# Correlation copies on two engines, a top-k choice in two pieces, and the next queries' turn behind the outputs

## The chip, the cores and the metric

The kernel runs on one core of a Trainium2 chip. The core has five engines that take their instructions in order and wait for each other through semaphores: TensorE (PE in the profile, with its weight loads shown apart as PEld), VectorE (DVE), ScalarE (ACT), GpSimd (POOL) and SyncE (SP), which here only issues DMAs. The metric is the device time of one execution in microseconds (us).

## The reference

The input x is 8 batches of 128 tokens with 512 features, and there is a context of the same shape. Two decoder layers run, each of three sublayers; after every one the input is added and layer-normalised:

```python
x = _layernorm(x + _L0_attn_ref(x, ...))       # 32 heads of 16, causal, with biases
x = _layernorm(x + _L0_xattn_ref(x, ctx, ctx)) # autocorrelation, 8 heads of 64
x = _layernorm(x + _L0_ffn_ref(x, ...))        # 28 experts of rank 8, the best 2
x = _layernorm(x + _L1_attn_ref(x, ...))       # 32 heads, q and k layer-normalised, ALiBi
x = _layernorm(x + _L1_xattn_ref(x, ctx, ...)) # 16 query heads on 4 key heads of 96
x = _layernorm(x + _L1_ffn_ref(x, ...))        # routed low-rank sum
```

The second of these is the one that the first two parts of the change touch. For every feature it takes the circular correlation of queries and keys over the 128 tokens, picks the 9 largest values of the 128, and adds the values shifted by the places found, weighted by a softmax:

```python
corr = jnp.fft.ifft(qf * jnp.conj(kf), axis=2).real
w, idx = jax.lax.top_k(corr.transpose(0, 1, 3, 2), topk)
w = jax.nn.softmax(w, axis=-1)
for i in range(topk):
    g = jnp.minimum(idx[:, :, None, :, i] + pos, L - 1)
    out = out + w[:, :, None, :, i] * jnp.take_along_axis(v, g, axis=2)
```

The fourth (second attention, `_L1_attn_ref`) is the one that the third part touches.

## The kernel before

Everything is in fp32. One batch is one tile: 128 tokens on the partitions and 512 features along them. The Tile framework's list scheduler takes the program in its order of issue and sets the order of the instructions on each engine by their dependencies, priorities and costs; on the chip each engine then works through its own list in order. What stands in which order in the source therefore shifts several lists at once.

**First attention, 0 to 225 us.** Batches go in pairs, four pairs of four groups of eight heads: sixteen steps (p, f), n = 0 to 15 (L515). A step computes scores (s_a L165), adds the causal mask (e_a L370, two instructions, one for each half of the rows), takes maxima (m_a L182) and exponentials (`exps`, L194) in two halves. Then the step before the previous one gives its outputs (`turned.out()`, o_a L244 and L250, into oT L258), the queries and keys of the next step are projected, the previous step's exponentials are transposed (`prev.turn()`, pt_a L225, copied as pT_a L226), and a piece of the correlation is done (`auto`, L505). Output projections (po, L86) and the layer norms stand in between.

**The correlation.** Class `Correlated` handles a pair of batches. `spectra` makes the products of the spectra, `correlate` transforms them back (pc L418, on a pair of PSUM banks) and copies them (co L423); `chosen(h)` finds for batch h of the pair the nine largest of 128 in each of four rows with MAX8 and MATCH_REPLACE8 (top, wk, nxt, L434 to L440) and makes the softmax weights (ex, su, rcw, L441 to L449); `shifted(h)` transposes the weights (wT, through pt_wT L129) and multiplies spectra (pvf L459, pw L463, wf L468, vw L471 and L473); `done(h)` transforms back (poc) and adds and normalises (x_c). The pieces of the pairs 0 and 1 are spread over places (n, 0) and (n, 1) of the attention's steps, two places a step, pair p from step 7 + 4p on (L500 to L503). Those of the pairs 2 and 3 (`third`, `fourth`) stand in a hand-written list among the experts (L716 to L761, 225 to 345 us).

**Second attention, 345 to 500 us.** A loop over the batches b (L832), each in two halves f = 0 and f = 2. A half computes scores, adds the ALiBi bias (e_a L703), takes maxima and exponentials (`exps(0)`, `exps(1)`), lets the previous half give its outputs (`turned.out()`), makes the next batch's raw queries (q L648), values or keys, transposes the previous half's exponentials, and divides (`divide`, rc_a L205 on VectorE, e_a L208 on GpSimd). For f = 2 `turned_queries(b + 1)` turns the next batch's normalised queries (q L652): four transposes into one PSUM bank (pTq L676) and four ScalarE activations that scale and shift (qT L678). `turned_tokens` makes the transposed tokens xTa (L139). The projection of the previous batch ends in x_a (L103), its layer norm comes later (`late`, L107).

Cross-attention and the last sublayer follow from 500 us on; the change does not touch their source.

Of the kernel before, what the change touches and what calls it, by code (L numbers as in the profile page):

```python
# [11 lines left out]
F32 = mybir.dt.float32  # L12
# [5 lines left out]
P = 128  # L18
B, S, D = 8, 128, 512
NC = D // P  # L20
# [8 lines left out]
BIG = -1e30  # L29
# [9 lines left out]
def bc(ap, shape):  # L39
    return ap.to_broadcast(shape)  # L40
# [3 lines left out]
def decoder(ctx: ExitStack, tc: tile.TileContext, a: dict, out: bass.AP):  # L44
    nc = tc.nc
# [4 lines left out]
    sm = ctx.enter_context(tc.tile_pool(name="sm", bufs=4))  # L50
# [3 lines left out]
    def stage(name, bufs, side=None):  # L54
        return tc.tile_pool(name=name, bufs=bufs, side=side, reuse_waits="tile")

    def bank(name):
        return ps1.tile([P, 512], F32, tag="ps1", name=name)

    def banks(name):  # L60
        return ps2.tile([P, 2, 512], F32, tag="ps2", name=name)
# [55 lines left out]
    def catch_up(behind=None):  # L117

        with tc.issue_after(behind.ins) if behind and late else nullcontext():
            while late:  # L120
                late.pop(0)()
# [161 lines left out]
    cp = autos.enter_context(stage("c0", 1, side="right"))  # L283
# [59 lines left out]
    def values(p, j):  # L343
        v, vd = vs[p, j] = v_bufs[(2 * p + j) % 4]
        pv = bank(f"pv0_{p}_{j}")
        mm_acc(pv, [(xts[p][:, c, j * P : (j + 1) * P], wv[:, c, :]) for c in range(NC)])
        by_head = lambda t: t.rearrange("p (a x d) -> p a x d", x=2, d=HD)
        nc.vector.tensor_tensor(padded(v), by_head(pv), by_head(bqkv[:, 0, :]), ALU.add)
        first_keys(vd, v)
# [33 lines left out]
    class Correlated:  # L383
# [27 lines left out]
        def correlate(self):  # L411
            pc = banks(f"pc_{self.p}")
            for i in range(NC):
                cols = slice(i * P, (i + 1) * P)
                for n in range(2):
                    for h in range(2):
                        rows = slice(64 * h, 64 * h + 64)
                        nc.tensor.matmul(  # L418
                            pc[:, h, cols], lhsT=self.pr[n][rows, 0, cols],
                            rhs=dft[rows, T_I + n * P : T_I + (n + 1) * P], start=(n == 0), stop=(n == 1),  # L420
                        )
            self.co = cp.tile([P, 2, NC, P], F32, tag="co", name=f"co_{self.p}")
            nc.scalar.copy(self.co.rearrange("p h c t -> p h (c t)"), pc)  # L423

        def chosen(self, h):

            b, co = self.bs[h], self.co[:, h]

            top = sm.tile([P, NC, 8], F32, tag="top", name=f"top_{b}")
            nxt = sm.tile([P, NC, 8], F32, tag="nxt", name=f"nxt_{b}")  # L430
            wk1 = cp.tile([P, NC, P], F32, tag="wk1", name=f"wk1_{b}")
            wk2 = cp.tile([P, NC, P], F32, tag="wk2", name=f"wk2_{b}")
            for i in range(NC):
                nc.vector.max(top[:, i, :], co[:, i, :])  # L434
                nc.vector.match_replace(wk1[:, i, :], top[:, i, :], co[:, i, :], BIG)
                nc.vector.max(nxt[:, i, :], wk1[:, i, :])

            nc.vector.memset(nxt[:, :, TOPK - 8 :], BIG)
            for i in range(NC):
                nc.vector.match_replace(wk2[:, i, :], nxt[:, i, :], wk1[:, i, :], BIG)  # L440
            ex = cp.tile([P, NC, P], F32, tag="ex", name=f"ex_{b}", bufs=2)  # L441
            nc.gpsimd.tensor_tensor(ex, co, bc(top[:, :, 0:1], [P, NC, P]), ALU.subtract)
            nc.scalar.activation(ex, ex, AF.Exp)
            nc.vector.scalar_tensor_tensor(ex, wk2, BIG, ex, ALU.is_equal, ALU.mult)
            su = sm.tile([P, NC], F32, tag="su", name=f"su_{b}")
            nc.vector.tensor_reduce(su, ex, AX.X, ALU.add)
            rc = sm.tile([P, NC], F32, tag="rcw", name=f"rcw_{b}")
            nc.vector.reciprocal(rc, su)
            nc.gpsimd.tensor_tensor(ex, ex, bc(rc.unsqueeze(2), [P, NC, P]), ALU.mult)  # L449
            self.ex[h] = ex  # L450
# [32 lines left out]
        def pieces(self):  # L483

            return [
                [self.spectra], [],
                [self.correlate], [lambda: self.chosen(0)],
                [lambda: self.shifted(0)], [lambda: self.chosen(1)],
                [lambda: self.done(0), lambda: self.shifted(1)], [],
                [lambda: self.done(1)],  # L490
            ]


# [21 lines left out]
    for n, (p, f) in enumerate(steps):  # L515
        if f == 0:
            oTs.append(ap.tile([P, 2, NC, P], F32, tag="oT", name=f"oT0_{p}"))
        qT, kbd = qk
# [117 lines left out]
    def turned_tokens(b):  # L636
        xT = qp.tile([P, NC, P], F32, tag="xT", name=f"xTa1_{b}")
        transposed(xs[b], NC, P, xT, f"xTa1_{b}", "a")
        return xT

    def normed(i, b, xT, later=None):


        n, w = (("q", w1q), ("k", w1k))[i]
        pq = bank(f"p{n}1_{b}")
        mm_acc(pq, [(xT[:, c, :], w[:, c, :]) for c in range(NC)])
        q = qp.tile([P, D], F32, tag=n, name=f"{n}1_{b}")
        nc.vector.tensor_scalar(q, pq, 8.0, -8.0, ALU.min, ALU.max)  # L648
        mean, rs = moments(q, f"{n}1_{b}")

        def normalized():
            done = nc.vector.tensor_scalar(q, q, mean, rs, ALU.subtract, ALU.mult)  # L652
            if i:
                nc.gpsimd.tensor_tensor(q, q, lnv[:, 0, :], ALU.mult)
                nc.gpsimd.tensor_tensor(q, q, lnv[:, 1, :], ALU.add)
            return done

        if later is None:
            normalized()
        else:  # L660
            later.append(normalized)
        return q
# [9 lines left out]
    def turned_queries(b, q):  # L672
        qT = ap.tile([P, NC, P], F32, tag="qT", name=f"qT1_{b}")
        pt = bank(f"pTq1_{b}")
        for c in range(NC):
            nc.tensor.transpose(pt[:, c * P : (c + 1) * P], q[:, c * P : (c + 1) * P], ident)  # L676
        for c in range(NC):
            nc.scalar.activation(  # L678
                qT[:, c, :], pt[:, c * P : (c + 1) * P], AF.Identity, scale=lnq[:, 0, c : c + 1], bias=lnq[:, 1, c : c + 1]
            )  # L680
        return qT
# [19 lines left out]
    def alibi_bias(f):  # L701
        def bias(e, s, r0):
            return nc.vector.tensor_tensor(e, s, alibi[:, f // 2, r0], ALU.add)  # L703

        return bias
# [43 lines left out]
    raw = [normed(i, 0, xT) for i in range(2)]  # L749
# [82 lines left out]
    for b in range(B):  # L832
        qT, kbd = qk
        v_now = v
        oT = ap.tile([P, NC, P], F32, tag="oT", name=f"oT1_{b}")
        for f in (0, 2):
            units = []
            for i in (f, f + 1):
                feats = slice(i * P, (i + 1) * P)
                units.append((qT[:, i, :], kbd[:, :, feats], v_now[0][:, i * 192 : (i + 1) * 192], v_now[1][:, i * 128 : (i + 1) * 128]))  # L840
            now = Heads16(ap, units, alibi_bias(f), oT[:, f : f + 2, :], f"a1_{b}_{f}", keys_late)
            if f == 2 and b + 1 < B:

                qT = turned_queries(b + 1, raw[0])
            now.exps(0)
            catch_up(now.scored)

            if turned:
                turned.out()
            if b + 1 < B:  # L850
                if f == 0:
                    raw = [normed(0, b + 1, xT)]
                else:
                    v = values(b + 1, xT)
                    if b + 2 < B:
                        xT = turned_tokens(b + 2)
            if b == 0:
                E(7) if f == 0 else None
            if b == B - 1:
                front.go(1)  # L860
            if prev:
                prev.turn()
            now.divide(0)
            now.exps(1)
            half = projection(b - 1, oT_before) if f == 2 and b else iter((0, 0))
            next(half)
            if b + 1 < B:
                if f == 0:
                    raw.append(normed(1, b + 1, xT, keys_late))
                else:  # L870
                    qk = qT, turned_keys(b + 1, raw[1])
            now.divide(1, turned_keys.done if f == 2 and b + 1 < B else None)
            if b == B - 1:
                front.go(1)
            next(half)
            turned, prev = prev, now
        oT_before = oT
# [12 lines left out]
    with stage("x1b", 2, side="right") as ap, stage("f1", 2, side="right") as fp:  # L890
# [164 lines left out]
        nxt, upcoming = Front(1), None  # L1055
# [41 lines left out]
        for b in range(B):  # L1097
            pr, j = divmod(b, 2)
            if j == 0 and b:
                front, nxt = nxt, upcoming  # L1100
# [222 lines left out]
```

## Time and profile before

| | us |
|---|---|
| median of 3 runs | 887.82 (887.67 to 888.66) |
| the profiled execution | 888.51 |
| its span, first to last instruction | 886.7 |
| TensorE busy in the span | 852.5 |
| VectorE busy | 562.8 |
| ScalarE busy | 370.2 |
| GpSimd busy | 189.0 |

The profile is that of one execution. Its span leaves out 1.8 us that lie around the first and the last instruction. The list of waits puts each wait of an engine down to the instruction that ended it. The chain of waits goes back from the last instruction of a stretch, at each step to what released it or to the instruction before it on its engine. In the timeline a row is one or several instructions of the same kind, with start, length, engine and line, what it writes and reads, and in brackets the idle time of the engine before it with what ended it. The granted clock (PEclk) is 1.00 at full speed; the mean over the span is 0.995.

### The profile page before, as it was taken

To read this page: it belongs to the slowest core of one execution; us is meant where nothing else is said; L and a number is where in the kernel's file an instruction comes from. 1 tells how busy PE (TensorE), PEld (TensorE's weight loads), DVE (VectorE), ACT (ScalarE), POOL (GpSimd) and SP (SyncE) were. 2 spreads that over 40 slices of the span, in tenths; PEclk is the share of its full clock that TensorE was granted. 3 is DMA by queue.
4 is the path that set the end of the run, shared out by engine and by line. 5 is a ranking of instruction groups with operands and counts; after the bars stand their busy time and mean duration, and the time that the engine had idled before them with its cause. 6 is when DMAs were issued, how large, how long until landed. Compare 5 with 4: busy or idle time off the path is not lost.

```text
span 886.7 us, 16971 instructions
## 1 busy us (share of the span) xinstructions
PE 852.5 (96%) x6454; PEld 524.6 (59%) x6454; DVE 562.8 (63%) x1329; ACT 370.2 (42%) x1534; POOL 189.0 (21%) x267
## 2 busy tenths in 40 slices
PE   9999999999899999999999999999999999999996
PEld 5766655754445454555555688758475846576442
DVE  3756797776968658788888621735363545467654
ACT  3787474564222116766666603213122322224310
POOL 2400233132243224555555300000000000000000
PEclk9999999999999999999999999999999999999998
DMA  9800000130300002000004020332113211313340
GB/s 331 322 2 25 2 13 13 49 108 1 131 0 25 1 0 96 2 1 2 2 1 143 27 72 1 70 89 45 41 36 92 45 47 36 82 42 78 83 94 35
DMA packets 30067, 50.68 MB, mean 57 GB/s; under 512 B 5537, under 2 KB 22049, under 8 KB 28193
## 3 DMA queue, kind: packets, MB, share of 16 engines
q1 hardware_dynamic: 27424, 47.49, 18.0%
q10 hardware_dynamic: 2560, 2.10, 1.1%
q8 instruction: 51, 0.84, 0.4%
q14 instruction: 32, 0.25, 0.1%
HBM read 30.69 MB, written 2.10 MB: 37 GB/s over the span
## 4 chain that ended last, share of the span: by engine, by line
PE 63%; DVE 20%; ACT 11%; POOL 2%; issue 1%; DMA 1%; SPq 0%; ACTq 0%; POOLq 0%; DVEq 0%
PE pqx L86 9%; PE pox L974 8%; ACT e_a L194 7%; PE pkx L86 4%; PE pvx L86 4%; PE s_x L912 4%; PE pof L86 4%; PE o_x L957 4%; PE pq L86 3%; PE pk L86 3%; DVE e_a L703 3%; PE pv L86 3%; DVE m_a L182 3%; PE pt_a L225 2%; PE pw L463 1%
## 5 line engine op out<-in xcount | busy, mean ns | idle before, releaser
L194 ACT ACTIVATE e_a<-e_a,m_a 128x128 f32<-128x128 f32 (+1 forms) x512 | 184.7, 364 | 93.6 <-DVE m_a L182 93.6
L933 ACT ACTIVATE e_x<-s_x,m_x 128x256 f32<-128x256 f32 x128 | 58.7, 484 | 140.2 <-DVE m_x L923 122.8
L194 ACT ACTIVATION_READ_ACCUMULATOR e_a<-e_a,m_a 128x1 f32 x512 | 96.8, 189 | 0.0
L974 PE MATMUL pox<-w_X_o,oTx 128*128 128x512 f32 x192 | 84.9, 596 | 1.0 <-DVE oTx L963 1.0
L86 PE MATMUL pqx<-xTx,w_X_q 128*128 128x256 f32 x384 | 84.9, 380 | 0.0
L86 PEld LDWEIGHTS pqx<-xTx,w_X_q 128*128 128x128 f32 x384 | 72.6, 190 | 11.4 <-issue 1.8
L922 DVE TENSOR_REDUCE m_x<-s_x 128x4 f32<-128x1024 f32 x32 | 37.6, 1217 | 41.2 <-PE s_x L912 41.2
L974 PEld LDWEIGHTS pox<-w_X_o,oTx 128*128 128x128 f32 x192 | 35.7, 190 | 46.4 <-issue 44.3
L182 DVE TENSOR_REDUCE m_a<-e_a 128x4 f32<-128x512 f32 (+1 forms) x128 | 62.6, 541 | 0.0
L97 POOL TENSOR_TENSOR rs_x<-ve_x,neghalf 128x1 f32<-128x1 f32 x7 | 3.8, 549 | 269.4 <-DVE ve_x L95 250.4
L208 POOL TENSOR_TENSOR e_a<-e_a,rc_a 128x512 f32<-128x512 f32 x64 | 51.8, 827 | 44.0 <-DVE rc_a L205 19.9
L225 PE MATMUL pt_a<-ident,e_a 128*128 128x128 f32 x384 | 48.7, 274 | 4.9 <-DVE e_a L370 3.9
L225 PEld LDWEIGHTS pt_a<-ident,e_a 128*128 128x128 f32 x384 | 43.4, 140 | 12.9 <-DVE e_a L370 4.9
L912 PE MATMUL s_x<-kTx,qTx 32*128 32x256 f32 x768 | 50.0, 385 | 1.0 <-ACT e_x L933 1.0
L912 PEld LDWEIGHTS s_x<-kTx,qTx 32*128 32x128 f32 x768 | 39.0, 184 | 17.1 <-issue 11.7
L957 PE MATMUL o_x<-pT_x,vx 128*32 128x512 f32 x384 | 43.7, 595 | 1.8 <-issue 0.6
L941 DVE STREAM_TRANSPOSE e_x<-e_x 128x1024 f32<-128x1024 f32 x32 | 39.7, 1241 | 0.8
L940 DVE TENSOR_SCALAR e_x<-e_x,rc_x 128x256 f32<-128x256 f32 x128 | 36.3, 347 | 4.2 <-DVE rc_x L937 2.5
L103 DVE TENSOR_TENSOR x_x<-pox,x_a 128x512 f32<-128x512 f32 x7 | 4.8, 686 | 52.5 <-PE pox L974 52.5
L823 ACT COPY qTx<-pqx 128x512 f32<-128x512 f32 x24 | 14.1, 595 | 55.5 <-PE pqx L86 55.5
L165 PEld LDWEIGHTS s_a<-kbd,qT 32*64 32x64 f32 x1024 | 20.7, 131 | 27.7 <-issue 12.7
L165 PE MATMUL s_a<-kbd,qT 32*64 32x256 f32 (+1 forms) x1024 | 33.2, 335 | 2.1 <-DVE pT_a L226 1.1
(223 smaller groups left out, 1611.8 us busy)
## 6 DMA issues: line engine op xcount, KB each, us to landing
pT_x<-e_x SPq DMA_DIRECT2D x224, 64.0 KB, 2.0
w_X_q<-in_X_q SPq DMA_DIRECT2D x3, 1024.0 KB, 4.8
w_X_o<-in_X_o SPq DMA_DIRECT2D x3, 1024.0 KB, 4.7
w_L_Wv<-in_L_Wv SPq DMA_DIRECT2D x2, 1024.0 KB, 6.3
w_L_Wo<-in_L_Wo SPq DMA_DIRECT2D x2, 1024.0 KB, 7.5
x_in<-in_x SPq DMA_DIRECT2D x8, 256.0 KB, 8.2
ct<-in_ctx SPq DMA_DIRECT2D x8, 256.0 KB, 4.4
cT<-in_ctxT SPq DMA_DIRECT2D x4, 512.0 KB, 4.0
```

The costliest lines, as they stand in the source:

```text
L86: nc.tensor.matmul(ps, lhsT=l, rhs=r, start=(i == 0), stop=(i == n - 1))
L165: nc.tensor.matmul(s[r // 2][64 * u : 64 * u + 64, r % 2, cols], lhsT=qT[rows, 64 - 64 * part : P - 64 * part], rhs=kbd[rows, :, :keys], s ...
L182: self.scored = nc.vector.tensor_reduce(self.m[:, part, rs, :], self.by_heads(part)[:, rs], AX.X, ALU.max, negate=True)
L194: nc.scalar.activation(e[:, r, x, :], e[:, r, x, :], AF.Exp, bias=self.m[:, part, r, x : x + 1], accum_out=self.su[:, part, r, x : x + 1],)
L208: nc.gpsimd.tensor_tensor(e, e, bc(self.rc[:, part, rs, :].unsqueeze(3), list(e.shape)), ALU.mult)
L225: nc.tensor.transpose(pt[:, r, cols], self.e[:, 2 * i + r, cols], ident)
L912: nc.tensor.matmul(sc[g // 2][:, g % 2, u * 256 : (u + 1) * 256], lhsT=qT[rows, (h0 + u) * NS + n, :], rhs=kT[rows, n], start=(n == 0), st ...
L922: nc.vector.tensor_reduce(m, self.s[i], AX.X, ALU.max, negate=True)
L933: nc.scalar.activation(self.e[:, :, j, :], self.s[half][:, i, :].rearrange("p (a k) -> p a k", k=32), AF.Exp, bias=self.m[:, j : j + 1], s ...
L941: nc.vector.transpose(self.e[:, :, js, :], self.e[:, :, js, :])
L957: nc.tensor.matmul(po[32 * g : 32 * g + 32, :], lhsT=v[:, s, g * XD + 32 * n : g * XD + 32 * n + 32], rhs=pT[:, s].rearrange("p i h x -> p ...
L974: nc.tensor.matmul(po, lhsT=oT[:, n, h * P : (h + 1) * P], rhs=w, start=(i == 0), stop=(i == NX - 1))
```

## The change

It has three parts. The copy of the correlations, one ScalarE instruction for both batches of a pair, becomes two: VectorE copies the first batch's half, ScalarE the second's. `chosen` is cut into `first_largest(h, 0)`, which handles two of the four rows, and `rest_chosen(h)`, which does the other two and all that follows; for the pairs 0 and 1 these pieces, and those after them, are spread over ten places instead of nine. And in the second attention `turned_queries` is issued behind `exps(0)`, `catch_up` and `turned.out()` instead of ahead of them.

```diff
@@ -420,20 +420,33 @@
                             rhs=dft[rows, T_I + n * P : T_I + (n + 1) * P], start=(n == 0), stop=(n == 1),
                         )
             self.co = cp.tile([P, 2, NC, P], F32, tag="co", name=f"co_{self.p}")
-            nc.scalar.copy(self.co.rearrange("p h c t -> p h (c t)"), pc)
-
-        def chosen(self, h):
+            co = self.co.rearrange("p h c t -> p h (c t)")
+            nc.vector.tensor_copy(co[:, 0], pc[:, 0])
+            nc.scalar.copy(co[:, 1], pc[:, 1])
+
+        def first_largest(self, h, half):
 
             b, co = self.bs[h], self.co[:, h]
-
-            top = sm.tile([P, NC, 8], F32, tag="top", name=f"top_{b}")
-            nxt = sm.tile([P, NC, 8], F32, tag="nxt", name=f"nxt_{b}")
-            wk1 = cp.tile([P, NC, P], F32, tag="wk1", name=f"wk1_{b}")
-            wk2 = cp.tile([P, NC, P], F32, tag="wk2", name=f"wk2_{b}")
-            for i in range(NC):
+            if half == 0:
+                self.top = sm.tile([P, NC, 8], F32, tag="top", name=f"top_{b}")
+                self.nxt = sm.tile([P, NC, 8], F32, tag="nxt", name=f"nxt_{b}")
+                self.wk1 = cp.tile([P, NC, P], F32, tag="wk1", name=f"wk1_{b}")
+            top, nxt, wk1 = self.top, self.nxt, self.wk1
+            for i in range(2 * half, 2 * half + 2):
                 nc.vector.max(top[:, i, :], co[:, i, :])
                 nc.vector.match_replace(wk1[:, i, :], top[:, i, :], co[:, i, :], BIG)
                 nc.vector.max(nxt[:, i, :], wk1[:, i, :])
+
+        def chosen(self, h):
+
+            self.first_largest(h, 0)
+            self.rest_chosen(h)
+
+        def rest_chosen(self, h):
+            self.first_largest(h, 1)
+            b, co = self.bs[h], self.co[:, h]
+            top, nxt, wk1 = self.top, self.nxt, self.wk1
+            wk2 = cp.tile([P, NC, P], F32, tag="wk2", name=f"wk2_{b}")
 
             nc.vector.memset(nxt[:, :, TOPK - 8 :], BIG)
             for i in range(NC):
@@ -484,10 +497,10 @@
 
             return [
                 [self.spectra], [],
-                [self.correlate], [lambda: self.chosen(0)],
-                [lambda: self.shifted(0)], [lambda: self.chosen(1)],
-                [lambda: self.done(0), lambda: self.shifted(1)], [],
-                [lambda: self.done(1)],
+                [self.correlate], [lambda: self.first_largest(0, 0)],
+                [lambda: self.rest_chosen(0)], [lambda: self.shifted(0), lambda: self.first_largest(1, 0)],
+                [lambda: self.rest_chosen(1)], [lambda: self.done(0)],
+                [lambda: self.shifted(1)], [lambda: self.done(1)],
             ]
 
 
@@ -839,14 +852,14 @@
                 feats = slice(i * P, (i + 1) * P)
                 units.append((qT[:, i, :], kbd[:, :, feats], v_now[0][:, i * 192 : (i + 1) * 192], v_now[1][:, i * 128 : (i + 1) * 128]))
             now = Heads16(ap, units, alibi_bias(f), oT[:, f : f + 2, :], f"a1_{b}_{f}", keys_late)
-            if f == 2 and b + 1 < B:
-
-                qT = turned_queries(b + 1, raw[0])
             now.exps(0)
             catch_up(now.scored)
 
             if turned:
                 turned.out()
+            if f == 2 and b + 1 < B:
+
+                qT = turned_queries(b + 1, raw[0])
             if b + 1 < B:
                 if f == 0:
                     raw = [normed(0, b + 1, xT)]
```

## The prediction

> **What bounds the kernel now.** I read the profile's first part, then the waits of TensorE by stage, then the chain of waits inside one stage, then the timeline around the lines that the change moves.
>
> ```profile
> span 886.7 us, 16971 instructions
> PE 852.5 (96%) x6454; PEld 524.6 (59%) x6454; DVE 562.8 (63%) x1329; ACT 370.2 (42%) x1534; POOL 189.0 (21%) x267
> ```
>
> TensorE is busy 96% of the span, and by that alone it would be the bound everywhere. The 34 us in which it is not busy lie mostly at the two ends and at few places between. Its waits from 95 to 230 us (first attention with the pairs 0 and 1 of the correlation) and from 345 to 495 us (second attention) hold the two places that the change touches; columns are total, times, longest:
>
> ```profile
> PE pt_a L225 <- DVE e_a L370: 3.9, 2, 2.0
> ...
> PE pTq L676 <- DVE q L652: 3.2, 6, 0.6
> ```
>
> The chain of waits of one batch of the second attention (432.84 to 455.03, a period of 22.19 us) says otherwise than the 96%: it holds VectorE, ScalarE and GpSimd, and no TensorE at all.
>
> ```profile
> 435.26 3.75 ACT e_a L194 x20
> 439.01 0.47 ACT xTa L139
> 439.48 0.78 ACT e_a L194 x4
> 440.26 0.68 ACT pT_a L226
> 440.94 1.34 ACT e_a L194 x8
> 442.29 0.02 issue
> 442.31 0.20 DVE rc_a L205
> ```
>
> From 435.26 to 442.29 ScalarE has no gap: its exponentials set when VectorE may divide. The timeline of ScalarE and VectorE there shows where each had slack (the bracket is the idle time before, and who ended it):
>
> ```profile
> 431.79 1.51 ACT L678 ACTIVATE qT<-pTq,lnq 128x128 f32<-128x128 f32 x4 [1.97 <-PE pTq L676]
> 435.26 0.40 ACT L194 ACTIVATE e_a<-e_a,m_a 128x128 f32<-128x128 f32 x1 [1.96 <-DVE m_a L182]
> ```
> ```profile
> 464.50 0.20 DVE L205 RECIPROCAL rc_a<-su_a 128x8 f32<-128x8 f32 x1 [0.95 <-ACT e_a L194]
> ```
>
> The last line is the rc_a of 442.31 one period later. The four activations of the next queries (qT) stand in a hole of 1.97 + 1.51 + 1.96 us: they cost nothing where they are.
>
> **The queries' turn behind the outputs, in second attention.** It removes nothing. On TensorE the 4 transposes pTq change places with the 24 matrix products into o_a, in the six batches 1 to 6 (in batch 0 there is no earlier output to go behind). Before, TensorE stood 0.61 us for the normalised q; after, o_a (453.87 to 454.68, 0.80 us) fills that, and pTq starts at 453.28 - 0.61 + 0.80 = 453.47, 0.19 us later. o_a comes 0.66 us earlier, but VectorE's order is unchanged and it fetches o_a only behind m_a. So on TensorE a gap of 0.61 x 6 = 3.7 us (3.2 in the waits list) is filled.
>
> ScalarE gets another order, which the built programs show: two qT, the eight exponentials of the first half, the other two qT, the copy xTa, two exponentials, the copy pT_a, and so on. The first two still lie in the hole. The other two now stand inside the unbroken stretch: 2 x 1.51 / 4 = 0.75 us. Behind them wait xTa (0.47), the second half's exponentials and pT_a; and for these waits VectorE's rc_a, which had been idle 0.95 us for them already, so nothing there absorbs it. Late next by 0.75: x_a, e_a L703 of the next batch, its m_a, its sums, POOL's e_a and rs_q, q L652, and with it the next period: the chain closes on itself. TensorE has 21.58 us of work in 22.19 and takes no part in it. 6 x 0.75 = +4.5 us. Bounds: all four on the path, 9.0; TensorE the bound, -3.7; the hidden case, 0.
>
> Here a rule speaks for the change. The Trainium skill, "Perfetto Trace Analysis" (Optimization Strategies), wants TensorE kept as highly used as possible and the engine it waits for optimised; by that, filling the 0.61 gap is worth -3.2 to -3.7. The same page (Identifying the Most-Contended Engine) distrusts matmul busy time as a measure, and the weight loads are busy 59%. The chain, which has no TensorE in it, decides: +4.5.
>
> **The copy of the correlations.** One ScalarE copy of 128x1024 becomes a VectorE copy of the first batch's half and a ScalarE copy of the second's.
>
> ```profile
> 102.39 1.00 ACT L423 COPY co<-pc 128x1024 f32<-128x1024 f32 x1
> 103.43 0.49 DVE L434 MAX8 top<-co 128x8 f32<-128x128 f32 x2 [0.64 <-ACT co L423]
> ```
>
> In the built program the ScalarE half waits for the VectorE half, so they run in series. The nearest rows are the 128x512 reads of a bank: 0.60 (L348/L668 on VectorE), 0.56 (xTa L139 on ScalarE). The first batch's choice can begin after 0.60 instead of 1.00, the second's after 1.16. VectorE is loaded with 0.60 x 4 = 2.4 us more; ScalarE relieved of 0.44 x 4. For pair 2 in the expert stage VectorE is full from 229 to 245 and the old copy lay hidden before that: +0.6. For pair 3 VectorE waited 0.40 for the copy: +0.2 for the copy, and -0.7 for the new order (one maximum fewer ahead of rcw, the transposes of the weights ahead of pvf). Together 0, bounds -0.7 and +1.2; the rest of that stage is a chain of TensorE.
>
> **The choice in two pieces, over ten places.** Before, TensorE stands twice for the second masked score:
>
> ```profile
> 112.31 0.88 PE L225 MATMUL pt_a<-ident,e_a 128*128 128x128 f32 x6 [1.96 <-DVE e_a L370]
> 174.89 0.95 PE L225 MATMUL pt_a<-ident,e_a 128*128 128x128 f32 x6 [1.96 <-DVE e_a L370]
> ```
>
> VectorE had put ex 0.60, m_a 0.60, su 0.60, m_a 0.32 and rcw 0.10 between the two e_a (108.27 and 111.33). After the change the two e_a are neighbours and the second ends at about 109.75 instead of 112.17: both stalls go, 3.9 us. What comes instead I walked through by hand, instruction by instruction in the new order with the durations of the old rows. For pair 0: the output projection waits 0.9 for oT of the step before, the transposes of the weights 0.85 for POOL's ex, s_a 0.6 for vw; at the scores of step (2,3) the walk is 1.6 ahead. Then the normalisation of the first batch of the pair, which waits for POOL's rs, stands on VectorE ahead of the scores' e_a (135.95 instead of 133.7), pvf waits 1.5 for pT_a, and the pair ends +0.4. For pair 1 it is likewise 1.6 ahead at its step (3,3), but there no queries, keys and values of a next step are left to fill: pt_a waits 2.0 for exponentials, pvf 2.5 for pT_a, the next pt_a 1.7 for the copy wf. The stage's last matmul comes at 219.6 instead of 217.4: +2.2, which holds both pairs. Bounds: -1 (half of the new waits are absorbed) and +3.5 (they do not overlap).
>
> TensorE's granted clock after the second of the old stalls, in stretches of 1 us (columns: span, its length, then each engine, then PEclk):
>
> ```profile
> 176.00:177.00 1.00, 1.00 (x7) 1.00 (x6) 1.00 (x3) 1.00 (x6) 0.00 (x0) 0.50 0.00 0
> 177.00:178.00 1.00, 1.00 (x3) 0.33 (x3) 1.00 (x5) 1.00 (x4) 0.00 (x0) 0.50 0.00 0
> ```
>
> It is 0.78 in 175 to 176 and 0.52 in 178 to 179: 3.2 us at half speed, 1.6 us of work lost, of which 0.7 came through (pair 1 took 0.69 longer than pair 0 over the same places). The Trainium skill, "TensorE: Matmul & The Clock Gate" (Why this matters for your kernels), asks for no gaps above some 3 us; by it a stall of 1.96 costs itself alone. The row says that one such stall did precede half speed, and the equal one of pair 0 did not. By the rule 0, by the row -0.7 when the stall goes, and +0.7 to +1.6 for each new stall of 2 us or more, of which the tail has two. I take 0 for the balance and leave it in the range.
>
> **The sum.** +4.5 + 0 + 2.2 = +6.7; against the profiled execution's 888.51 (span 886.7 and 1.8 around it) 895.2. That execution is 0.69 above the median of the runs, so the median goes from 887.82 to 894.5. I round down to 894.0, because the walk through the first attention counts more new waits than it can have found relief for.
>
> **Rivals.**
> - TensorE is the bound in second attention, as 96% suggests, and the two stalls of 1.96 go without successors: -3.5 - 3.9 + 0, about 880.5. For it: the waits of 0.61 are the only ones there. Against it: the chain, and rc_a's 0.95. It decides if VectorE's rc_a has over 0.75 us of cover that the timeline does not show. The second half of it alone, with the queries' turn hidden, gives 884.
> - Second attention hides the two activations (an order that ScalarE's waits absorb), the first attention's gains and new waits balance: 888 to 889.5. For it: the copies in series do not bring what they say. Against it: no gap in ScalarE from 435.26 to 442.29.
> - The new waits of the first attention do not overlap and the tail falls to half clock: 4.5 + 3.5 + 1.6 = +9.6, about 897.5. For it: two stalls over 2 us in the tail; against it: pair 0's stall of 1.96 cost no clock.
>
> **How the numbers follow.** Likeliest case (+4.5, and the first attention between -1 and +3.5) 0.62, its own range 891 to 896.5; hidden 0.12; long 0.14; TensorE-bound, or the first attention winning outright, 0.12. 0.2% is 1.8 us (886.0 to 889.6), about what a measurement of this kernel can tell from no change. Faster 0.12 from the first rival; the same 0.10 from the hidden case; slower 0.78 from the rest. The range leaves out the first rival and the far end of the third: 887.0 to 898.0.
>
> **What would show it.** In second attention the period should be 22.94 instead of 22.19; qT in two groups of two, the second with no idle time before it; rc_a's idle 1.7 instead of 0.95; pTq's wait of 0.61 gone. In first attention both 1.96 waits for e_a L370 gone, new waits for POOL's ex, oT and pT_a, and the stage's end 2 us later. The prediction is wrong if the period stays at 22.2 (then the activations are hidden), falls to 21.6 (TensorE was the bound), or if the first stage ends earlier than 217.

## The result: slower by 1.7%

The changed kernel takes 903.42 us (median of 6 runs, 900.75 to 906.61); the kernel before, in the same comparison, 888.51 (6 runs, 887.67 to 888.83). The ratio is 1.017, with a 95% interval of 1.015 to 1.019: 14.9 us slower. The forecast was 894.0, range 887.0 to 898.0: the sign is right, the size is not.

The profiled execution took 906.61, 3.2 above the median of its runs. Of that, 2.0 us are not the change's: the first projection ran at half speed from its first instruction (pq 3.75 us instead of 1.96), and at 100 us the instructions still stand 1.99 later than in the profile of before. Of the profiles below one has the same start (pq 3.75 in the last kernel); in the others full speed comes sooner. The first part of the page:

```profile
span 904.8 us, 16973 instructions
PE 860.4 (95%) x6454; PEld 526.1 (58%) x6454; DVE 565.3 (62%) x1333; ACT 368.6 (41%) x1534; POOL 188.7 (21%) x267
```

TensorE is busy 7.9 us longer with the same 6454 matmuls: that is mostly time at half clock. The other 10 us by which the span is longer are idle time. Where they lie, from the starts of the same instruction in both timelines:

| instruction | before | after | shift | added in this stretch |
|---|---|---|---|---|
| pc of pair 0 | 99.57 | 101.56 | +1.99 | 2.0, the start |
| pc of pair 1 | 162.15 | 166.52 | +4.37 | 2.4, pair 0 |
| pc of pair 2 | 225.22 | 237.94 | +12.72 | 8.3, pair 1 |
| pTq of batch 0 | 321.64 | 334.60 | +12.96 | 0.2, expert stage |
| pTq of batch 7 | 475.47 | 491.92 | +16.45 | 3.5, second attention |
| first pqx | 524.74 | 543.51 | +18.77 | 2.3, its last batch |

TensorE's waits in the first attention and, in the last line, in the second (total, times, longest):

```profile
PE pt_a L225 <- DVE e_a L370: 2.4, 1, 2.4
PE pvf L472 <- DVE ve_a L95: 2.2, 1, 2.2
PE po L86 <- DVE oT L258: 1.9, 2, 1.0
PE pt_a L225 <- ACT wf L482: 1.6, 1, 1.6
PE poc L86 <- POOL vw L485: 1.2, 1, 1.2
...
PE pTq L689 <- DVE q L665: 4.6, 5, 0.9
```

The two waits of 1.96 for e_a are gone, as the change would have it. In their place stands a longer list. The longest ones lie together at the end of pair 1; TensorE's timeline there:

```profile
205.26 1.74 PE L225 MATMUL pt_a<-ident,e_a 128*128 128x128 f32 x12 [2.36 <-DVE e_a L370]
...
209.82 2.54 PE L472 MATMUL pvf<-ct,dft 128*128 128x512 f32 x4 [2.16 <-DVE ve_a L95]
212.15 3.06 PE L476 MATMUL pw<-wT,dft 128*128 128x512 f32 x4
216.81 0.87 PE L225 MATMUL pt_a<-ident,e_a 128*128 128x128 f32 x6 [1.59 <-ACT wf L482]
218.92 2.07 PE L86 MATMUL poc<-vw,dft 128*128 128x512 f32 x2 [1.24 <-POOL vw L485]
```

The list puts pvf's wait down to ve_a, which pvf does not read; VectorE's copy pT_a, just ahead of ve_a, ended at 209.77, and in another trace below the same wait is put down to that copy.

pw takes 3.06 here and 1.88 to 1.99 elsewhere. The stretches of 1 us say why (the number after POOL's is the granted clock):

```profile
212.00:213.00 1.00, 1.00 (x2) 0.34 (x1) 0.00 (x0) 1.00 (x7) 0.00 (x0) 0.50 0.00 0
...
219.00:220.00 1.00, 1.00 (x2) 0.42 (x2) 0.00 (x0) 0.00 (x0) 1.00 (x1) 0.50 0.00 0
221.00:222.00 1.00, 1.00 (x15) 0.83 (x16) 0.00 (x0) 0.00 (x0) 0.00 (x0) 0.50 0.00 0
```

The clock is halved from 211 to 214.5 and from 218 to 225. A third such stretch comes at 511.5 to 515, behind a wait of 1.61 at the end of the second attention.

In the second attention the chain of waits of one period now has the two activations in it:

```profile
450.31 2.98 ACT e_a L194 x16
453.29 0.69 ACT qT L691 x2
453.98 0.47 ACT xTa L139
454.45 0.78 ACT e_a L194 x4
455.23 0.68 ACT pT_a L226
455.92 2.12 ACT e_a L194 x12
458.03 0.02 issue
458.05 0.20 DVE rc_a L205
```

And in ScalarE's timeline qT stands in two groups, the first in the old hole, the second with no idle time before it:

```profile
446.85 0.81 ACT L691 ACTIVATE qT<-pTq,lnq 128x128 f32<-128x128 f32 x2 [1.97 <-PE pTq L689]
450.31 0.40 ACT L194 ACTIVATE e_a<-e_a,m_a 128x128 f32<-128x128 f32 x1 [2.66 <-DVE m_a L182]
453.20 0.79 ACT L691 ACTIVATE qT<-pTq,lnq 128x128 f32<-128x128 f32 x2
```

The period, from the rc_a at 458.05 to the one a batch later at 480.94, is 22.89 us; before, it was 22.19.

### The profile page after: what moved, and what is told of

The parts are those of the page before. It is cut to its first block, busy times and chain, and to the rows that moved or that the text cites. A ratio compares the mean times of both kernels' runs of the same rounds, so it can differ in the third digit from the quotient of the medians.

```text
span 904.8 us, 16973 instructions
## 1 busy us (share of the span) xinstructions
PE 860.4 (95%) x6454; PEld 526.1 (58%) x6454; DVE 565.3 (62%) x1333; ACT 368.6 (41%) x1534; POOL 188.7 (21%) x267
## 4 chain that ended last, share of the span: by engine, by line
PE 59%; DVE 22%; ACT 13%; POOL 2%; issue 1%; DMA 1%; SPq 1%; ACTq 0%; POOLq 0%; DVEq 0%
PE pqx L86 9%; ACT e_a L194 9%; PE pox L987 8%; PE pkx L86 4%; PE pvx L86 4%; PE pof L86 4%; PE s_x L925 4%; PE o_x L970 4%; DVE m_a L182 3%; DVE e_a L716 3%; PE pq L86 3%; PE pk L86 2%; PE pv L86 2%; PE pw L476 2%; PE poc L86 2%; DVE e_a L370 2%
## 5 line engine op out<-in xcount | busy, mean ns | idle before, releaser
L165 PE MATMUL s_a<-kbd,qT 32*64 32x128 f32 (+1 forms) x1024 | 33.7, 334 | 3.1 <-DVE pT_a L226 2.2
```

Of the source, the lines that this page charges most:

```text
L165: nc.tensor.matmul(s[r // 2][64 * u : 64 * u + 64, r % 2, cols], lhsT=qT[rows, 64 - 64 * part : P - 64 * part], rhs=kbd[rows, :, :keys], s ...
```

## The experiments

Each expectation below sets a theory A against rivals with letters of their own. Theory A after the result: the queries' turn costs what two activations cost on ScalarE's unbroken stretch; the rest is lost by the pieces of the choice, in pair 0 and in the tail of pair 1, part of it as half clock. The runs of before that each kernel is compared with were taken beside it: medians 887.94 for the first four kernels, 889.09 for the next six, 889.20 for the last two.

### Each part alone

The queries' turn alone:

```diff
-            if f == 2 and b + 1 < B:
-                qT = turned_queries(b + 1, raw[0])
             now.exps(0)
             catch_up(now.scored)
             if turned:
                 turned.out()
+            if f == 2 and b + 1 < B:
+                qT = turned_queries(b + 1, raw[0])
```

> The kernel before with the third part alone (the queries' turn behind the outputs). Theory A, two activations in ScalarE's unbroken stretch: the six periods of second attention grow by 0.70 each, +4.2 us, about 892.5; the first attention as before, with its two stalls of 1.96. Rival B, TensorE is the bound and the third part helps while the others hurt: -3, about 885.5. Rival C, the third part costs little by itself and the growth of the periods in the changed kernel comes with its lower clock: within 1 us of before.

Measured: 892.48 us, +4.5 (ratio 1.0047, 1.003 to 1.0064). Theory A holds; B and C fall. TensorE's wait for q did not go: it is 4.6 us (5 times, longest 0.9) instead of 3.2. The outputs fill the old gap, and q comes later still. In this trace the last batch also has half clock (497.5 to 501), behind a wait of 1.62.

The copies alone:

```diff
-            nc.scalar.copy(self.co.rearrange("p h c t -> p h (c t)"), pc)
+            co = self.co.rearrange("p h c t -> p h (c t)")
+            nc.vector.tensor_copy(co[:, 0], pc[:, 0])
+            nc.scalar.copy(co[:, 1], pc[:, 1])
```

> The kernel before with the first part alone (the correlations copied half by VectorE, half by ScalarE). Theory A: a copy of 0.65 more on VectorE four times, hidden or balanced: within 1 us of before. Rival D, VectorE is what the first attention waits for, and the two copies in series stand in its way: 4 x 1.2 = up to +5 us, or the stalls of 1.96 each longer by 0.65.

Measured: 887.74 us, -0.2 (0.9997, 0.9988 to 1.0006): no change. The waits of 1.96 did not grow, as D had it, but fell to 1.71 each, and no half clock follows the second. Among the experts, where pair 2's choice begins, the waits barely change (1.76, 1.36 and 0.68; before 1.65, 1.29 and 0.68), but in this execution half clock comes behind them and takes back what was gained. pw, 1.98 before, takes 3.58:

```profile
236.81 3.58 PE L465 MATMUL pw<-wT,dft 128*128 128x512 f32 x4 [0.68 <-ACT wT L139]
```

D falls.

The choice in two pieces over ten places, alone: the change's second part, with the single ScalarE copy kept.

```diff
-                [self.correlate], [lambda: self.chosen(0)],
-                [lambda: self.shifted(0)], [lambda: self.chosen(1)],
-                [lambda: self.done(0), lambda: self.shifted(1)], [],
-                [lambda: self.done(1)],
+                [self.correlate], [lambda: self.first_largest(0, 0)],
+                [lambda: self.rest_chosen(0)], [lambda: self.shifted(0), lambda: self.first_largest(1, 0)],
+                [lambda: self.rest_chosen(1)], [lambda: self.done(0)],
+                [lambda: self.shifted(1)], [lambda: self.done(1)],
```

> The kernel before with the second part alone (the choice in two pieces, the pieces over ten places, one copy as before). Theory A: nearly all of what the changed kernel loses in the first attention: +10 us, about 898.5, with one to three stretches of half clock after 205 us; its runs scatter by several us, those of before by one. Rival D: the copies carry the loss, and this is within 2 us of before.

Measured: 896.24 us, +8.3 (1.0097, 1.0082 to 1.0112). Theory A had +10; most of the loss in the first attention is here, and D falls.

Both first parts, the queries' turn left at its old place:

```diff
+            if f == 2 and b + 1 < B:
+                qT = turned_queries(b + 1, raw[0])
             now.exps(0)
             catch_up(now.scored)
             if turned:
                 turned.out()
-            if f == 2 and b + 1 < B:
-                qT = turned_queries(b + 1, raw[0])
```

> The changed kernel with the queries' turn back at its old place (first and second part). Theory A: the sum of parts, 14.9 less 4.2, +10.7 us, about 899. Rival C, the third part costs nothing by itself: about 903, as the changed kernel. If the parts do not add up, the rest is their common effect on the clock.

Measured: 897.14 us, +9.2 (1.0103, 1.0084 to 1.0122). With the +4.5 of the third part this makes 13.7 of the 14.9 us; the 1.2 left over are within what the runs of these kernels scatter by. C falls. TensorE's timeline at the end of pair 1, and one of the stretches of half clock there:

```profile
203.89 1.78 PE L225 MATMUL pt_a<-ident,e_a 128*128 128x128 f32 x12 [2.35 <-DVE e_a L370]
...
208.45 3.78 PE L472 MATMUL pvf<-ct,dft 128*128 128x512 f32 x4 [1.49 <-DVE ve_a L95]
...
215.63 0.88 PE L225 MATMUL pt_a<-ident,e_a 128*128 128x128 f32 x6 [1.59 <-ACT wf L482]
217.74 1.12 PE L86 MATMUL poc<-vw,dft 128*128 128x512 f32 x2 [1.24 <-POOL vw L485]
...
222.65 1.94 PE L396 MATMUL pa<-x_a,dft 128*64 128x512 f32 x8 [0.67 <-ACT pT_a L226]
```
```profile
211.00:212.00 1.00, 1.00 (x2) 0.34 (x1) 0.00 (x0) 1.00 (x7) 0.00 (x0) 0.50 0.00 0
```

### Where in the first attention

Pair 1 back on its nine places, pair 0 on the ten:

```diff
         def pieces(self):
+            if self.p:
+                return [
...
+                    [self.correlate], [lambda: self.chosen(0)],
+                    [lambda: self.shifted(0)], [lambda: self.chosen(1)],
+                    [lambda: self.done(0), lambda: self.shifted(1)], [],
...
```

> First and second part, with pair 1 on its nine old places and pair 0 on the ten new ones. Theory A: the tail, where the last pieces of pair 1 lie one place later with no further step to cover them, carries most of the loss; what is left is pair 0's 2.4 us: about 890.3, the four waits after 203 us (pt_a 2.35, pvf 1.49, pt_a 1.59, poc 1.24) and the half clock after them gone. Rival D: cutting the choice costs the same in each pair: half of 9.2 is left, 892.5 or more.

Measured: 892.36 us, +3.3 (1.0037, 1.0023 to 1.0051). Pair 1 on the ten places thus carries 9.2 - 3.3 = 5.9 us. The four waits after 203 us are gone, and the profile shows full clock from 10 to 880 us. The edit takes back the cut of the choice and the tenth place together; no run keeps the cut on nine places, so which of the two costs is not shown. What is left is pair 0; its profiled execution shows +2.4 at the pc of pair 1, as the changed kernel does. By the runs alone rival D (892.5) was not excluded; the place of the shift in the trace decides: pair 1 adds nothing (pc of pair 1 +2.35, of pair 2 +1.63).

In pair 0 of the changed kernel VectorE's timeline shows the layer norm of batch 0 with two waits ahead of the masked scores, whose matmuls were done by 136.9:

```profile
136.13 0.69 DVE L103 TENSOR_TENSOR x_c<-poc,x_a 128x512 f32<-128x512 f32 x1 [0.67 <-PE poc L86]
...
138.63 0.55 DVE L107 TENSOR_SCALAR x_c<-x_c,mv_c,rs_c 128x512 f32<-128x512 f32 x1 [0.67 <-POOL rs_c L97]
139.09 1.82 DVE L370 TENSOR_TENSOR e_a<-s_a,masks 128x768 f32<-128x768 f32 x2
```

At the end of pair 1 the norm of that pair's first batch stands in the same place, ahead of scores whose matmuls were done by 202.1:

```profile
203.79 0.55 DVE L107 TENSOR_SCALAR x_c<-x_c,mv_c,rs_c 128x512 f32<-128x512 f32 x1 [0.67 <-POOL rs_c L97]
204.26 1.81 DVE L370 TENSOR_TENSOR e_a<-s_a,masks 128x768 f32<-128x768 f32 x2
```

In pair 0 TensorE has the next step's pq and pk to work on meanwhile; here it has nothing, and stands 2.36 us for these scores. No run moves the norm in pair 1, so that its share of the tail is read from the trace alone.

The next kernel is the one just shown, pair 1 on its old places, with the norm of batch 0 issued behind the scores:

```diff
-            xs[b] = add_norm(xs[b], po, f"c0_{b}")
+            xs[b] = add_norm(xs[b], po, f"c0_{b}", late if self.p == 0 and h == 0 else None)
```

> The kernel with pair 1 on its old places (first and second part otherwise), with one more edit: the layer norm of batch 0 after the correlation (x_c) is issued behind the next step's scores instead of ahead of them. Theory A, this norm with its waits for poc and for GpSimd holds back the masked scores e_a of step (2,3) and with them the pair: most of pair 0's 2.4 us comes back, so within 1 us of before, e_a of that step near 136.5 instead of 138. Rival I, the loss of pair 0 lies in the later pieces (its transposes of weights, pvf, poc): as without this edit, +2.4 to +3.3 us.

Measured: 890.74 us, +1.65 (1.0016, 1.0005 to 1.0027). In the trace the pc of pair 1 stands +0.55 instead of +2.35, so the norm held 1.8 of the 2.4 us; by the runs it is 3.3 - 1.65 = 1.6. The masked scores there:

```profile
134.08 0.69 DVE L103 TENSOR_TENSOR x_c<-poc,x_a 128x512 f32<-128x512 f32 x1 [0.68 <-PE poc L86]
134.92 1.82 DVE L370 TENSOR_TENSOR e_a<-s_a,masks 128x768 f32<-128x768 f32 x2
```

By its time this kernel misses "within 1 us": some of pair 0's loss is not the norm, and what it is was not tested.

### The waits of 1.96 without the rest

The kernel before, with only the end of the choice (ex, su, rcw) issued one place later, so that the masked scores are neighbours:

```diff
-                [self.correlate], [lambda: self.chosen(0)],
-                [lambda: self.shifted(0)], [lambda: self.chosen(1)],
-                [lambda: self.done(0), lambda: self.shifted(1)], [],
+                [self.correlate], [lambda: self.picks(0)],
+                [lambda: self.weights(0), lambda: self.shifted(0)], [lambda: self.picks(1)],
+                [lambda: self.weights(1), lambda: self.done(0), lambda: self.shifted(1)], [],
```

> The kernel before with the end of the choice (ex, su, rcw) issued one place later, so that the two masked scores of the next step are neighbours on VectorE, for the pairs 0 and 1; nothing else moves. Theory A: both waits of 1.96 go, and the weights come 1 to 1.5 later, which costs 0.5 to 1.5 at pt_wT: -1 to -3 us in all, 885 to 887, and no half clock near 175. Rival F: the wait only moves to the transposes of the weights: within 0.5 us of before.

Measured: 893.35 us, +4.3 (1.0053, 1.0032 to 1.0075). Both theories fall. The waits of 1.96 are gone; each is replaced by a longer one, for a pair of PSUM banks that VectorE's copy pT_a gives free, now behind the two masked scores, four maxima, oT, ex and kbd:

```profile
114.77 2.52 PE L467 MATMUL pvf<-ct,dft 128*128 128x512 f32 x4 [3.20 <-DVE pT_a L226]
...
179.79 2.68 PE L467 MATMUL pvf<-ct,dft 128*128 128x512 f32 x4 [3.20 <-DVE pT_a L226]
```

And behind both, the clock is halved (in this profile also at 242.5 to 246, among the experts):

```profile
117.00:118.00 1.00, 1.00 (x6) 0.99 (x6) 0.86 (x6) 0.61 (x4) 0.87 (x1) 0.50 0.00 0
...
182.00:183.00 1.00, 1.00 (x5) 0.83 (x5) 0.86 (x6) 0.62 (x4) 0.89 (x1) 0.50 0.00 0
```

### What sets the period of the second attention

TensorE's, VectorE's and GpSimd's orders of before; only two activations are held behind the exponentials:

```diff
-                qT = turned_queries(b + 1, raw[0])
+                qT, second_half = turned_queries(b + 1, raw[0], True)
...
+            if second_half:
+                with tc.issue_after(now.last_exp.ins):
+                    second_half()
```

`second_half` issues the activations of the third and fourth block.

> The kernel before with TensorE's, VectorE's and GpSimd's orders unchanged; only the last two of the four query activations are made to stand behind the first half's exponentials on ScalarE, as in the changed kernel. Theory A: the same loss as the third part alone, +4.2 to +4.5 us, about 892.3. Rival B, the loss comes from TensorE's order (outputs ahead of transposes): 0, about 888.

Measured: 893.48 us, +4.4 (1.0048, 1.0036 to 1.006). The loss of the third part is in ScalarE's order alone.

The opposite: the outputs ahead on TensorE, all four activations ahead of the exponentials:

```diff
+            if f == 2 and turned:
+                turned.out()
             if f == 2 and b + 1 < B:
                 qT = turned_queries(b + 1, raw[0])
             now.exps(0)
             catch_up(now.scored)
-            if turned:
+            if f == 0 and turned:
                 turned.out()
```

> The kernel before with the outputs ahead of the queries' transposes on TensorE, as in the changed kernel, but all four activations ahead of the first half's exponentials on ScalarE. Theory A: TensorE's filled gap is worth nothing, 0 within 1 us, about 888, TensorE waiting elsewhere in the period. Rival B, TensorE is the bound: -3.2 us, about 884.7. Rival G, the order on TensorE is what costs: +4.

Measured: 888.83 us, -0.3 (0.9999, 0.999 to 1.0009). TensorE's filled gap is worth nothing: B falls, and G. In the trace TensorE's waits over the second attention add up to 5.0 us (for q 2.4, for k 1.7, for pT_a 0.9), and before it was 5.0 too (3.2, 1.2 and 0.6): they moved.

If ScalarE's stretch sets the period, work taken out of it must shorten it:

```diff
-        transposed(xs[b], NC, P, xT, f"xTa1_{b}", "a")
+        transposed(xs[b], NC, P, xT, f"xTa1_{b}", "v" if b > 1 else "a")
```

> The kernel before with the copy xTa of the second attention taken from ScalarE's unbroken stretch (0.47 us of its chain, six batches) to VectorE, where it falls beside waits of 0.47 and 0.84. Theory A, ScalarE's stretch sets the period: the period falls by up to 0.47 and the kernel gains 5 to 6 times that, -2.3 to -2.8 us. Rival B, TensorE bounds the period: at most -0.6 a period too, but with TensorE's waits for q gone; Rival H, VectorE bounds it: +0.6 a period, +3.5 us.

Measured: 886.94 us, -2.15 (0.9976, 0.9968 to 0.9984): faster than both kernels, though a little short of the gain expected. H falls. A period is 0.28 shorter, not 0.47. The chain of waits shows what took over: TensorE, whose wait for q is down to 0.3 a batch but not gone.

```profile
428.91 0.84 DVE q L652
429.74 0.04 issue
429.79 0.66 PE pTq L676 x4
430.45 0.36 PE o_a L244 x16
430.81 0.11 PE o_a L250 x8
430.92 0.22 PE o_a L244 x16
431.14 0.11 PE o_a L250 x8
431.25 3.63 PE pv L86 x8
434.88 0.44 PE pt_xTa L129 x4
435.32 1.31 PE pt_a L225 x12
...
440.50 0.85 PE s_a L165 x32
```

The 0.80 us of o_a stand on this chain, between pTq and pv. Now the changed kernel's order on TensorE ought to pay; the two edits together:

```diff
-        transposed(xs[b], NC, P, xT, f"xTa1_{b}", "a")
+        transposed(xs[b], NC, P, xT, f"xTa1_{b}", "v" if b > 1 else "a")
...
+            if f == 2 and turned:
+                turned.out()
             if f == 2 and b + 1 < B:
                 qT = turned_queries(b + 1, raw[0])
             now.exps(0)
```

> The two edits of the second attention together: xTa copied by VectorE, and the outputs ahead of the queries' transposes with all four activations ahead of the exponentials. With xTa moved, the chain of a period runs through TensorE (pTq, o_a, pv, pt_a, po, s_a) beside ScalarE's. Theory A: now the changed kernel's order on TensorE is worth something, the wait of 0.33 for q is filled and the period falls from 21.91 to between 21.6 and 21.7: -1.2 to -2 us more than xTa alone, -3.3 to -4 against before, about 885.3. Rival J, VectorE and GpSimd alone set the period of 21.91: no more than xTa alone, -2.1.

Measured: 885.93 us, -3.3 against before (0.996, 0.9947 to 0.9972). This is the fastest of these kernels. By medians it is 1.1 us beyond xTa alone (-3.3 against -2.15, each with its own runs of before); the intervals of the two overlap (0.9947 to 0.9972 and 0.9968 to 0.9984), so the runs alone do not exclude J. The trace does: TensorE's list there has no wait for q any more, and from the pTq of batch 1 to that of batch 7 it takes 127.6 us instead of 128.6 with xTa alone.

### All causes taken out

The changed kernel with the edits of the last kernel, pair 1 on its old places and the norm behind the scores:

```diff
+            if self.p:
+                return [
...
-            xs[b] = add_norm(xs[b], po, f"c0_{b}")
+            xs[b] = add_norm(xs[b], po, f"c0_{b}", late if self.p == 0 and h == 0 else None)
...
+            if f == 2 and turned:
+                turned.out()
...
+        transposed(xs[b], NC, P, xT, f"xTa1_{b}", "v" if b > 1 else "a")
```

> The changed kernel with every named cause taken out: pair 1 on its old places, the norm of batch 0 behind the scores, all four activations ahead of the exponentials, xTa on VectorE. Theory A: the causes add: 1.6 for the rest of pair 0, less the gain of the second attention (2 to 4), so 886 to 888.5, some 15 us below the changed kernel. If over 891, a cause is still unnamed.

Measured: 887.12 us, -2.1 against before (0.9971, 0.996 to 0.9983) and 16 us below the changed kernel. Part of that is the gain of the two edits in the second attention, which the kernel before lacks. Against the kernel before with these two edits (885.93) it is 1.2 us slower: so the named causes carry all but about 1 us of the loss, and what is left lies in the parts that stay, the copies and pair 0.

## Why the prediction was wrong

- **The queries' turn: right**, in mechanism and size. Forecast +4.5, measured +4.5 alone (and +4.4 for ScalarE's order alone). Two activations on the stretch were put at 0.75 us; they take 0.69 on the chain, and the period grew by 0.70, not 0.75: with six batches 4.2, which the trace of the activations alone shows (3.4 up to the pTq of batch 7 and 0.7 in the last batch). That the runs came to 4.5 is within their scatter. rc_a's idle time came to 2.06 instead of the 1.7 forecast, and pTq's wait did not vanish: TensorE waited 0.9 for a q that was itself late. The rule of keeping TensorE fullest would have said -3.2; the chain without TensorE in it was the better reader.
- **The copies: right** as a sum (0 forecast, -0.2 alone), with other terms than forecast. Pair 2, put at +0.6, took 0.26 longer where no half clock fell (from its pc to that of pair 3 39.33 us in the kernel with both first parts, 39.07 before). That both waits of 1.96 shrink by 0.25 was not forecast.
- **The choice over ten places: this step failed**, in the size of its terms. "+2.2, which holds both pairs", with +3.5 as its far end, stood against 9.2 measured with the copies. That the two waits of 1.96 go, and that waits for oT, ex, pT_a and wf come, was right. The profile with both first parts alone, where the pc of pair 2 comes 8.3 later once its late start is taken off, shows the mis-sized terms.
  - "The pair ends +0.4": pair 0 ended at +2.4. The walk saw the norm ahead of the scores but put the masked scores at 135.95; with the late start taken off they come at 139.09 - 1.99 = 137.1 in the changed kernel, after the norm's own waits for poc and rs_c. With that norm behind the scores 1.8 of the 2.4 were gone.
  - The three tail waits that the walk had (6.2 us) measure 2.35 + 1.49 + 1.59 = 5.4, and the first of them is for the masked scores, not for exponentials. But the walk left out poc's wait for vw (1.24) and pa's (0.67).
  - "I take 0 for the balance" of the clock: half clock lasts from 205.5 to 212.3, 6.8 us in which TensorE waits for 1.5, so some (6.8 - 1.5) / 2 = 2.7 us are lost. Against that stands the half clock of the kernel before at 175, which is gone here: pair 1 took 63.07 us there and 62.40 in the queries' turn alone, which has full clock at that place, so -0.7.
  - Together 2.0 + 1.9 - 0.8 + 2.7 - 0.7 = 5.1, an estimate, of the 6.1 by which that trace exceeds the +2.2. For the other 1.0 the cause stays open.
- **The clock.** The forecast weighed a row (half clock behind one of two waits of 1.96) against the Trainium skill, "TensorE: Matmul & The Clock Gate" (Why this matters for your kernels: no gaps above about 3 us), and took neither. Over nine profiles, the kernel before among them, a lone wait of 1.92 to 1.97 at this place was followed within 2 us by half clock in 4 of 15 cases. Behind the waits of 3.20 it came in 2 of 2, as the page would have it. Behind the tail's wait of 2.35 it came in 2 of 3 profiles, and in the third, the changed kernel's, behind the 2.16 that follows. The waits of 1.61 and 1.62 at the end of the second attention had it behind them both. The page's bound is thus not a safe one here: waits well under 3 us cost clock in some profiles and none in others. What decides between them no run shows.
- **The rival** with longer waits and a tail at half clock had the right mechanism, at 897.5, and too small a size and chance.

## What to carry to other kernels

Ask first whether the engine whose gap an edit fills is on the chain of waits: here the same reorder on TensorE was worth nothing, and about 1 us once the chain had been moved onto TensorE. Before pieces of work are spread over one more place, ask what covers the last of them: at the end of this stage nothing did, and in all three profiles with the new tail half clock came behind its waits. Twice a reorder on VectorE removed the waits of 1.96 here, and both times the waits that came in their place were longer in sum: look for them before counting the gain.

## What had not been expected

- Removing only the two waits of 1.96 made the kernel 4.3 us slower: a bank pair's release slid behind four maxima and a 3.20 us wait took its place, with half clock behind it.
- At the start of an execution the matmuls run at half speed for a varying time: in the profile of before up to about 5 us, in that of the changed kernel up to about 9.5 (seen from their durations; the column of the granted clock shows 1.00 there). This shifted everything after it by 2.0 us, more than many a change is worth.
- The changed kernel's runs scatter more: 900.75 to 906.61 in 6 runs, against 887.09 to 891.21 in the largest set of before (35 runs). That half clock hits by chance behind its waits is a likely reason; the timed runs have no traces to show it.
